# A graph layer on one Trainium2 core: message slots that run on from block to block, with a second product at each block's end

## The chip, the cores and the metric

The kernel runs on one core of a Trainium2 chip. A core has five engines that run their own instruction streams: TensorE (PE, matrix products; its weight loads are shown apart as PEld), VectorE (DVE), ScalarE (ACT), GpSimd (POOL) and SyncE (SP, which here only issues transfers). Sixteen DMA engines move data between the chip's memory (HBM) and the core's working memory (SBUF). TensorE writes its products to a second, small memory (PSUM), which VectorE and ScalarE read. Instructions of different engines wait for one another by semaphores.

The metric is the time of one execution on the device in microseconds, the median of several runs. Lower is better.

## The reference, cut to what matters

All arrays are fp32. `x` has 12,500 nodes of 256 values; `src` and `dst` are 200,000 edges, sorted by `dst`. `dst` is drawn as floor(12500 u^2) with u uniform, so low nodes have many edges and high ones few.

```
xn = layernorm(x)
h = xn
for layer in 0, 1, 2:                      # weights Wl, Wr: 256 x 256
    s   = segment_sum(h[src], dst)         # sum of the messages of each node
    cnt = number of edges of each node
    h   = (s / max(cnt, 1)) @ Wl.T + bl + h @ Wr.T
    if layer < 2: h = leaky_relu(h, 0.01)
x = x + log_softmax(h) + linear_attention(xn)   # 4 heads of 32
x = x + moe(layernorm(x))                  # 8 experts, top 2, gelu, 256 wide
```

The part that the change touches is `segment_sum(h[src], dst)`: 200,000 rows of 256 values are fetched by index and added up by destination, three times.

## The kernel before

**Blocks, slots and the sums.** The nodes are cut into 98 blocks of 128. A *slot* is a list of up to 128 edges that all have their destination in one block. For each slot the kernel does three things: GpSimd issues an indirect DMA that fetches the 128 source rows of 1 KB into a message buffer (`gather`, L978); VectorE makes a 128 x 128 matrix of zeros and ones, edge against node of the block, four slots in one instruction (`make_hots`, L970); and TensorE multiplies that matrix with the messages and adds the result to the block's sums in PSUM (`product`, L993). The last slot of a block is padded with edges that point past the end, so the slots of a block begin anew with each block: with 98 blocks there are at most 1659 (`NS`). Blocks are taken in falling order, the last one (fewest edges) first.

**Which block a slot belongs to is data.** The program is written out for a fixed number of slots, and the place of a slot's sums comes from a table in SBUF (`where`, `where1`), which TensorE's sequencer reads into registers eight slots at a time (`addresses`, `AHEAD` = 8). The sums of 4 (layer 0) or 6 (layers 1 and 2) blocks are held in a ring in PSUM. When a block's sums are complete is not known when the program is written: `ends_by` (L88) gives, from the distribution of `dst` and a margin of 4.5 standard deviations, a slot number `due[r]` by which block r is surely done, and at that slot `take_up(r)` (L1004) has VectorE read its sums, divide by the counts, and clear the ring's place. `last = due[-1]` (L931) is 1626, so that many slots a layer are run. If the data breaks one of these bounds, a flag (`other`) sends the kernel down a slower branch, `one_by_one` (L888), which makes no assumption.

**The order in a layer** is written out by hand in `on_the_way_of` (L955; under `manual_schedule`): for each slot s, `gather(s)`, every fourth slot a `make_hots` for three groups of four ahead, `product(s)`, then loads of the previous results (`load_z`) and `take_up` where due, and then as much other work as a credit allows (`SHARE` = 0.7, 0.5 and 1.0 us of TensorE a slot in layers 0, 1 and 2). The other work is generators that yield their cost: in layer 0 the keys, values and context of the attention (`first_products`, which loads xn), in layer 1 the attention's output (`attended`, which loads xT), in layers 0 and 1 the products with the weights for the blocks taken up (`products`, `linear`), and in layer 2 the softmax, the router and the experts (`expert_steps`: p_h at L835, gelu L837, p_y L804). What is left when the slots are over runs behind the last product. The last group of layer 2 needs its own softmax (`softmaxed`) and transposes (p_tr, L519) before its experts.

**Message buffers.** There are `MSGS` = 32, each a tile of its own. Gather s writes buffer s mod 32 and may not start before the buffer's earlier readers are done. For slots from 32 on this is reduced to one wait every fourth slot, by hand:

```
            if s >= MSGS:
                last_reader = [made_of[s - MSGS + FEW - 1]] if s % FEW == 0 else []
```

(L981 to L982): gather s waits for the product of slot s - 29, and the rest of the dependencies that the framework would find are declared away. For the first 32 slots of a layer the framework's own dependencies stand, which with 32 separate tiles are those on the layer before.

**Setup.** Before the first layer, `edges`, a table of (source, destination) pairs, is written to HBM; samples of it, every 128th edge, are read back (`samp_i`), and from them the first edge of each block is searched for (p_lt, an indirect read `near`, p_st); counts of slots and their running sum give `where` (p_blk, L407 to L413). For 13 chunks of 128 slots, VectorE works out each slot's first edge, GpSimd fetches the 128 edges of each slot by an indirect DMA (`got`, L449), TensorE transposes sources and destinations (p_t), and VectorE copies them to `src_of` and `dst_of` (L457 to L459). Between these stand the layernorms of x (`first_norm`, L206), ten groups of four blocks before the tables and fifteen after, whose results go to HBM as the source of layer 0's gathers. Six more VectorE instructions on the `where` tables stand at the start of `on_the_way` (L938 to L944).

**Queues.** SyncE issues nearly all the loads and stores, in program order; ScalarE's queue carries the edge sources, the weights and the stores of the normed x; GpSimd's carries the indirect transfers.

## Time and profile before

| | value |
|---|---|
| median of 3 timed runs | 7560.73 us (7558.60 to 7565.72) |
| profiled execution, its own time | 6887.68 us |
| span in the profile | 6885.9 us |
| mean granted TensorE clock | 0.815 |
| TensorE busy | 5885.1 us, 85% |
| GpSimd busy | 4857.7 us, 71% |
| VectorE, ScalarE busy | 31%, 12% |
| HBM read and written | 765.16 MB, 130.01 MB |
| setup | 0 to 178 us |
| layer 0 | 178 to 2267 us |
| layer 1 | 2293 to 4393 us |
| layer 2 | 4414 to 6827 us |
| rest | 6827 to 6885.9 us |

The profiled execution is shorter than the timed ones; the parts of the table below the first row all belong to that one execution. The layers' borders are the first and the last gather of a layer for layers 0 and 1, and the last product for layer 2.

How to read the lines of the profile: a group of instructions has its source line, its engine, its operation, what it writes and reads (out<-in), the shape, and the count; then the busy time, the mean of one in ns, and the engine's idle time just before these instructions with what ended most of it. "issue" as the releaser means that the engine waited for nothing that the profile shows. In a table by stretches each row is a window of time with the busy time and number of instructions of each engine in it. In lists in order of time the columns are start, duration, engine, line, operation, and in brackets the idle time before it and its releaser. The granted clock (PEclk) is a share of TensorE's full speed.

### The profile page before, as it was taken

What the parts mean: (1) busy time and instruction counts of PE and PEld (TensorE: products, weight loads), DVE (VectorE), ACT (ScalarE), POOL (GpSimd) and SP (SyncE); (2) the same over time, 40 slices, a digit from 0 to 9 for tenths busy, and PEclk for the clock granted to TensorE, in tenths of its full rate; (3) what the DMA queues carried; (4) which work ended last, traced back from release to release, by engine and by line L of the source; (5) the groups of instructions that cost most, each with busy time, mean ns of one, the idle gap of its engine ahead of it and who ended that gap; (6) DMA issues with size and microseconds to landing.
All of it is one profiled execution on the core that took longest, in us unless ns stands there. A gap on an engine that the chain in (4) does not pass through costs nothing.

```text
span 6885.9 us, 59263 instructions
## 1 busy us (share of the span) xinstructions
PE 5885.1 (85%) x18905; PEld 3700.0 (54%) x18905; DVE 2139.6 (31%) x5121; ACT 850.9 (12%) x1444; POOL 4857.7 (71%) x5004
## 2 busy tenths in 40 slices
PE   1788888888889777788888888889999999999998
PEld 0566666443343445543344333366666667676776
DVE  7333333221111233322211111134434444343433
ACT  0111111000000000000000000022222222222221
POOL 1777777777777677777777777666666666666663
PEclk9999999676665788866666655589999999999999
DMA  6655555443333566644444333443434433333332
GB/s 189 186 162 168 168 172 165 121 120 112 112 111 104 150 185 183 190 137 120 121 120 122 112 107 108 107 121 117 125 116 126 119 113 115 118 113 110 108 110 62
DMA packets 477361, 899.44 MB, mean 131 GB/s; under 512 B 90244, under 2 KB 305805, under 8 KB 476803
## 3 DMA queue, kind: packets, MB, share of 16 engines
q0 software_dynamic: 234832, 641.49, 32.8%
q1 hardware_dynamic: 225110, 234.04, 10.6%
q10 hardware_dynamic: 17114, 19.99, 0.9%
q8 instruction: 174, 2.85, 0.2%
q14 instruction: 131, 1.07, 0.0%
HBM read 765.16 MB, written 130.01 MB: 130 GB/s over the span
## 4 chain that ended last, share of the span: by engine, by line
PE 54%; POOL 18%; issue 12%; DMA 11%; DVE 4%; ACT 1%; SPq 0%; DVEq 0%; POOLq 0%; ACTq 0%
PE acc L993 20%; POOL msg L978 18%; PE p_h L835 10%; PE p_y L804 10%; DMA msg<-y,src_of 7%; PE p_mm L191 4%; PE p_tr L519 2%; DMA xn<-y 2%; PE p_a L661 1%; PE p_l L537 1%; PE p_b L752 1%; PE p_z L597 1%; PE p_r L708 1%; PE p_k L570 1%; DMA xt<-in_x 1%
## 5 line engine op out<-in xcount | busy, mean ns | idle before, releaser
L978 POOL DMA_INDIRECT msg<-y,src_of x4878 | 4837.9, 992 | 1818.3 <-issue 1292.8
L993 PE MATMUL acc<-msg,hots 128*128 128x256 f32 (+1 forms) x9756 | 3601.7, 489 | 523.0 <-DMA msg<-y,src_of 416.8
L993 PEld LDWEIGHTS acc<-msg,hots 128*128 128x128 f32 x9756 | 2019.4, 230 | 2070.6 <-DMA msg<-y,src_of 1188.0
L970 DVE TENSOR_TENSOR hots<-cols,dst_of 128x512 f32<-128x512 f32 (+1 forms) x1221 | 842.1, 690 | 2990.3 <-PE acc L993 2989.3
L835 PE MATMUL p_h<-turned,w_sb 128*128 128x512 f32 (+1 forms) x1600 | 769.7, 606 | 0.0
L804 PE MATMUL p_y<-w_sb,hT 128*128 128x256 f32 x3136 | 741.1, 379 | 0.1
L804 PEld LDWEIGHTS p_y<-w_sb,hT 128*128 128x128 f32 x3136 | 595.8, 190 | 81.5 <-ACT hT L837 0.5
L521 ACT COPY turned<-p_tr 128x512 f32<-128x512 f32 (+1 forms) x250 | 142.8, 578 | 3333.9 <-PE p_tr L519 3312.2
L791 DVE SCALAR_TENSOR_TENSOR x<-p_y,comb,x 128x256 f32<-128x256 f32 x784 | 341.2, 476 | 576.8 <-PE p_y L804 576.8
L835 PEld LDWEIGHTS p_h<-turned,w_sb 128*128 128x128 f32 x1600 | 317.5, 199 | 221.5 <-issue 197.1
L837 ACT ACTIVATE hT<-p_h,b_sb 128x512 f32<-128x512 f32 (+1 forms) x400 | 271.6, 679 | 1173.0 <-PE p_h L835 1172.2
L191 PE MATMUL p_mm<-wlr_sb,turned 128*128 128x512 f32 x784 | 392.8, 629 | 0.3 <-ACT turned L521 0.2
L191 PEld LDWEIGHTS p_mm<-wlr_sb,turned 128*128 128x128 f32 x784 | 157.6, 203 | 127.3 <-issue 105.9
L1018 DVE SCALAR_TENSOR_TENSOR h<-acc,inv_w,h 128x256 f32<-128x256 f32 x196 | 94.7, 483 | 233.2 <-PE acc L993 229.8
L661 PE MATMUL p_a<-m_sb,xT 128*128 128x256 f32 x392 | 126.0, 479 | 24.2 <-DMA xT<-xT_tab 24.2
L519 PE MATMUL p_tr<-ident,xn 128*128 128x128 f32 x196 | 47.3, 401 | 113.7 <-DMA xn<-y 113.7
L180 DVE TENSOR_TENSOR yz<-p_mm,bl_sb 128x256 f32<-128x256 f32 x196 | 82.2, 419 | 194.6 <-ACT yz L179 194.6
L179 ACT COPY yz<-p_mm 128x256 f32<-128x256 f32 x196 | 73.0, 373 | 520.6 <-PE p_mm L191 506.4
L519 PE MATMUL p_tr<-ident,h 128*128 128x128 f32 x392 | 74.0, 319 | 71.0 <-DVE h L1028 45.1
L661 PEld LDWEIGHTS p_a<-m_sb,xT 128*128 128x128 f32 x392 | 97.8, 252 | 47.9 <-issue 25.3
L837 ACT ACT_TABLE_LOAD x70 | 89.8, 1283 | 230.0 <-PE p_h L835 229.1
L519 PEld LDWEIGHTS p_tr<-ident,h 128*128 128x128 f32 x392 | 55.5, 163 | 94.7 <-DVE h L1028 55.8
(197 smaller groups left out, 2251.7 us busy)
## 6 DMA issues: line engine op xcount, KB each, us to landing
msg<-y,src_of POOLq DMA_INDIRECT x4878, 2.8
h<-z SPq DMA_DIRECT2D x72, 512.0 KB
y<-yz SPq DMA_DIRECT2D x98, 256.0 KB
z<-yz SPq DMA_DIRECT2D x98, 256.0 KB
y<-o_norm ACTq DMA_DIRECT2D x24, 512.0 KB
xn<-y SPq DMA_DIRECT2D x24, 512.0 KB
xT_tab<-turned SPq DMA_DIRECT2D x24, 512.0 KB
z<-z SPq DMA_DIRECT2D x24, 512.0 KB
```

Of the source, the lines that this page charges most:

```text
L191: nc.tensor.matmul(p, hT[:, k, j * P:(j + 1) * P], w[:, k, :], start=(k == 0), stop=(k == 1))
L519: nc.tensor.transpose(p_tr[:, j * P:(j + 1) * P], t[:, j, k * P:(k + 1) * P], ident)
L521: nc.scalar.copy(tT[:, k, :n * P], p_tr[:, :n * P])
L661: nc.tensor.matmul(p[:, j - j0, :], xT[:, k, j * P:(j + 1) * P], m2_sb[:, k, :], start=(k == 0), stop=(k == 1))
L791: nc.vector.scalar_tensor_tensor(xt[:, j, :], p[:, j - j0, :], comb[:, j, i:i + 1], xt[:, j, :], op0=OP.mult, op1=OP.add)
L804: nc.tensor.matmul(p[:, j - j0, :], hT[:, k, j * P:(j + 1) * P], e.w2[:, i, k, :], start=(k == 0), stop=(k == 1))
L835: nc.tensor.matmul(p_h[:, :n * P], e.w1[:, i, k, m * P:(m + 1) * P], tT[:, k, :n * P], start=(k == 0), stop=(k == 1))
L837: nc.scalar.activation(hT[:, m, :n * P], p_h[:, :n * P], AF.Gelu, bias=e.b1[:, i, m:m + 1])
L970: nc.vector.tensor_tensor(hot[:, :n, :], cols.rearrange("p (o c) -> p o c", o=1).to_broadcast([P, n, P]), dst_of[:, s:s + n].rearrange("p ...
L978: got = nc.gpsimd.indirect_dma_start(out=msgs[s % MSGS][:, :D], out_offset=None, in_=y_tab[layer], in_offset=bass.IndirectOffsetOnAxis(ap= ...
L993: got = nc.tensor.matmul(acc[:, bass.ds(at[s % AHEAD], w)], hots.pop(s), msgs[s % MSGS][:, :w], start=False, stop=True, skip_group_check=True)
L1018: got = nc.vector.scalar_tensor_tensor(h, sums_of(r), inv[:, r:r + 1], h, op0=OP.mult, op1=OP.add)
```

## The change

**Slots run on.** A slot is now 128 consecutive edges of the sorted list, whichever blocks they belong to: `NSF` = 200000/128 rounded up = 1563 a layer, where 1626 were run. A slot belongs to the block of its first edge in the order of work. Where a block ends inside a slot, the edges of the next block in that slot are added by a second product: `make_hot_end(r)` builds a one-hot matrix of that slot against block r + 1 (VectorE, made some 8 slots ahead, three buffers), and `product_end(r)` multiplies it with the slot's messages into the sums of r + 1. Which slot that is is data too: the second product reads its messages at an address from a register (table `where_end`), so the message buffers are now one tile `msgs` with 48 places. There are 97 second products a layer, in the program behind the product of slot `due[r] - 1`, ahead of the taking up of that block.

**Bounds.** `due`, `lowest` and `highest` are worked out anew for such slots (`end_of`); the flag now checks three conditions for every slot: its block is at least `lowest`, at most `highest`, and at most one more than that of the slot before.

**Waits of the gathers.** From slot 48 on, a gather of every fourth slot waits for the product of the slots that last used its four buffers and, where a second product could have read them last (`first_reuse`), for that second product. Below slot 48 the framework's own dependencies stand, as before below 32.

**Tables.** Slots being consecutive edges, the edges of a chunk are read by one direct load on SyncE's queue, in reverse order of slots, and put in order by a product with a flipped identity in place of the transpose; the block of a slot is its first destination divided by 128. The tables `where` and `where_on` come from that by arithmetic on one row, the flag by three comparisons on one row, and the ends' tables from counts (p_nr, p_nc) and one indirect read (`end_got`). The search for the blocks' first edges, the per-slot block numbers and the 13 indirect reads now belong to the other branch (`slots_by_block`). `edges` has a block of padding in front as well. One of the two copies of each transposed piece is now ScalarE's. The memsets of `due_sb` on GpSimd become those of `lowest_sb` and `highest_sb`.

```diff
-MSGS = 32
+MSGS = 48
...
-    due = [min(ends_by(r + 1), NS) for r in range(NB)]
+    NSF = (E + P - 1) // P
+    due = [min(math.ceil(end_of(r + 1, 1)), NSF) for r in range(NB)]
...
+        for c in range(NCF):
+            n = min(P, NSF - c * P)
-            got = work.tile([P, P, 2], I32, name="got")
-            nc.gpsimd.indirect_dma_start(
-                out=got.rearrange("p c t -> p (c t)"), out_offset=None, in_=edges,
-                in_offset=bass.IndirectOffsetOnAxis(ap=of_i[:, 0:1], axis=0))
+            got = work.tile([P, P, 2], I32, name="got", bufs=4)
+            nc.sync.dma_start(got[:n], edges[P + E - P * (c * P + n):P + E - P * P * c, :]
+                              .rearrange("(q e) t -> q e t", e=P))
...
+            nc.scalar.copy(got_f[:n, 0, :], got[:n, :, 0])
...
+                nc.tensor.matmul(p_t[:, :n], got_f[:n, t, :], flip[:n, P - n:], start=True,
+                                 stop=True)
+                (nc.scalar.copy if t else nc.vector.tensor_copy)(to[:, c * P:c * P + n], p_t[:, :n])
+            p_row = psum.tile([1, P], F32, name="p_row", tag="p_sm")
+            nc.tensor.matmul(p_row[:, :n], ahead[:n, c:c + 1], flip[:n, P - n:], start=True,
+                             stop=True)
+            nc.vector.tensor_copy(row[:, c * P:c * P + n], p_row[:, :n])
...
+        nc.vector.tensor_copy(row_i, row[:, :NSF])
+        nc.vector.tensor_scalar(part, row_i, RING[0] - 1, None, op0=OP.bitwise_and)
+        nc.vector.tensor_scalar(where[:, :NSF], part, 2.0 * D, None, op0=OP.mult)
...
+        off = sort.tile([1, 3, NSF], F32, name="off")
+        nc.vector.tensor_tensor(off[:, 0], row[:, :NSF], lowest_sb, OP.is_lt)
+        nc.vector.tensor_tensor(off[:, 1], row[:, :NSF], highest_sb, OP.is_gt)
...
+        nc.vector.tensor_reduce(any_off, off.rearrange("p t s -> p (t s)"), AX.X, OP.max)
...
     def take_messages(lists, n):
 
-        msgs = [lists.tile([P, W], F32, name=f"msg{i}") for i in range(n)]
-        for msg in msgs:
-            nc.vector.memset(msg[:, D:], 1.0)
+        msgs = lists.tile([P, n, W], F32, name="msgs")
+        nc.vector.memset(msgs[:, :, D:], 1.0)
         return msgs
...
-        last = due[-1]
+        last = NSF
...
         def gather(s):
             got = nc.gpsimd.indirect_dma_start(
-                out=msgs[s % MSGS][:, :D], out_offset=None, in_=y_tab[layer],
+                out=msgs[:, s % MSGS, :D], out_offset=None, in_=y_tab[layer],
                 in_offset=bass.IndirectOffsetOnAxis(ap=src_of[:, s:s + 1], axis=0))
             if s >= MSGS:
-                last_reader = [made_of[s - MSGS + FEW - 1]] if s % FEW == 0 else []
+                last_reader = []
+                if s % FEW == 0:
+                    last_reader = [made_of[min(s - MSGS + FEW, last) - 1]]
+                    last_reader += [made_of[-1 - r] for r, f in enumerate(first_reuse)
+                                    if s <= f < s + FEW]
...
+        def make_hot_end(r):
+            ends[r] = work.tile([P, P], F32, name="hot_end", bufs=3)
+            nc.vector.tensor_scalar(ends[r], cols, dst_end[:, r:r + 1], None, op0=OP.is_equal)
+
+        def product_end(r):
+
+            nonlocal at_end
+            if r % AHEAD == 0:
+                at_end = addresses(where_end, r, NB, MSGS, PE, W)
+            got = nc.tensor.matmul(sums_of(r + 1), ends.pop(r),
+                                   flat[:, bass.ds(at_end[r % AHEAD], w)], start=False, stop=True,
+                                   skip_group_check=True)
+            tc.declare_no_dep(got.ins, group=evicts,
+                              reason="only blocks that are not yet taken up are added to")
+            tc.add_to_no_dep_group(products_at, got.ins)
+            made_of[-1 - r] = got.ins
...
             product(s)
+            for i in range(NB - 1):
+                if due[i] == min(s + 8, last):
+                    if i not in ends:
+                        make_hot_end(i)
+            for i in range(NB - 1):
+                if due[i] == s + 1:
+                    product_end(i)
```

## The prediction

> **What bounds the kernel now.** I read the costliest groups first, to see which two engines could set the end; then the busy time by stretches, cut at the layers; then the order of time on GpSimd and on TensorE at the layers' ends and starts.
>
> The costliest groups of the page (busy us, mean ns of one, then idle time before and its main releaser):
>
> ```profile
> L978 POOL DMA_INDIRECT msg<-y,src_of x4878 | 4837.9, 992 | 1818.3 <-issue 1292.8
> L993 PE MATMUL acc<-msg,hots 128*128 128x256 f32 (+1 forms) x9756 | 3601.7, 489 | 523.0 <-DMA msg<-y,src_of 416.8
> ```
>
> 4878 gathers are 3 x 1626. GpSimd's idle time is mostly "issue": between gathers it waits for nobody. The stretches of the three layers and of the end (busy us and instructions of each engine, granted TensorE clock, DMA share, GB/s):
>
> ```profile
> core 0: us, PE busy (x) PEld busy (x) DVE busy (x) ACT busy (x) POOL busy (x), PEclk, DMA share, GB/s
> 178.00:2267.00 2089.00, 1757.70 (x5767) 1085.43 (x5768) 554.83 (x1205) 170.28 (x343) 1592.28 (x1626) 0.79 0.48 141
> 2293.00:4393.00 2100.00, 1726.07 (x4216) 912.61 (x4216) 476.54 (x800) 63.81 (x144) 1604.71 (x1626) 0.70 0.47 138
> 4414.00:6827.00 2413.00, 2309.98 (x8651) 1647.59 (x8652) 960.26 (x2470) 583.96 (x884) 1639.72 (x1626) 0.93 0.39 115
> 6827.00:6886.00 59.00, 36.23 (x147) 29.25 (x146) 16.03 (x51) 16.92 (x31) 0.00 (x0) 0.80 0.06 18
> ```
>
> Layers 0 and 1 take the same time although their TensorE work differs (5767 against 4216 records): 2089/1626 = 1.285 and 2100/1626 = 1.292 us a slot. Layer 2 takes 1.48, with TensorE 96% busy at a clock of 0.93. GpSimd in order of time, at the end of layer 0:
>
> ```profile
> 2265.17 0.94 POOL L978 DMA_INDIRECT msg<-y,src_of  x1 [0.30 <-issue]
> 2266.42 0.95 POOL L978 DMA_INDIRECT msg<-y,src_of  x1 [0.30 <-issue]
> 2293.07 0.94 POOL L978 DMA_INDIRECT msg<-y,src_of  x1 [25.71 <-DMA z<-yz]
> ```
>
> 0.95 + 0.30 = 1.25 us a gather, and no wait but the one for the next layer's rows. So layers 0 and 1 are GpSimd's, layer 2 TensorE's, and the first 178 us are the tables'. How long a gather takes to land, and TensorE at a layer's quiet start, in its dense part, at layer 1's start and at the very end (records of a product come in pairs):
>
> ```profile
> DMA to landing us min/median/max: 2.6/2.8/8.7
> ```
>
> ```profile
> 4437.30 17.33 PE L993 MATMUL acc<-msg,hots 128*128 128x256 f32 x28 [0.17 <-DMA msg<-y,src_of]
> ...
> 4511.14 1.03 PE L993 MATMUL acc<-msg,hots 128*128 128x256 f32 x4
> ...
> 2321.11 3.75 PE L661 MATMUL p_a<-m_sb,xT 128*128 128x256 f32 x8 [5.23 <-DMA xT<-xT_tab]
> ...
> 6841.12 0.75 PE L519 MATMUL p_tr<-ident,o 128*128 128x128 f32 x2 [13.72 <-DVE o L171]
> ```
>
> A product takes 1.24 us (17.33/14) where TensorE follows the gathers, 0.43 where it is dense (4511.14 to 4512.00 is two).
>
> **What the Trainium skill says.** "TensorE: Matmul & The Clock Gate", Part 1: a little-used TensorE passes half its clock pulses; the 0.70 to 0.79 of layers 0 and 1 against 0.93 agree. "DMA: Bandwidth & Descriptors", Anatomy of one DMA: 2.0 us and bytes/436e3 for a transfer that GpSimd issues; an estimate of 2.3 us for 128 rows of 1 KB, where the trace has 2.8, which I use. "SBUF — State Buffer", Who interferes with whom: VectorE in its two-port modes shuts GpSimd out; the first gathers of layer 0 last 1.28, 2.65, 1.68 and 5.86 us while VectorE works without a gap (177 to 190 us).
>
> **The change, part by part.**
>
> *Gathers.* 1626 to 1563: 63 fewer a layer. Layers 0 and 1: 63 x 1.285 + 63 x 1.292 = -162 us. Layer 2: nothing, TensorE sets it.
>
> *Second products.* 97 a layer against 63 slots dropped: 34 more products. In layers 0 and 1 hidden under the gathers: TensorE has 332 and 374 us of idle time there, and a 1.24 us product speeds up as TensorE gets denser. In layer 2: 34 x 0.43 = +14.6. The extra 97 one-hots on VectorE (0.2 to 0.7 us each, from the 128x512 hots' 0.69) hide in a VectorE that is 23 to 40% busy. Without that cover, 97 x 0.69 = 67 us a layer.
>
> *A new wait.* The message buffer is now one tile, and the second product reads it at an address from a register, so it counts as a reader of all 48 messages. Gathers from slot 48 on are freed of this by a declaration; the first 48 are not (the branch begins at `s >= MSGS`). So the gathers of slots 8, 16, 25, 33 and 42 of each layer, those that follow a second product in the order of the program, wait for it. Each costs: landing of the gather before 2.8, its product 1.22, second product 1.22, start 0.3, less the usual 1.25: 4.3 us; at least 2.65 (0.67 and 0.43 for the products), at most 9.5 where TensorE stands before a late load of 5.2 us as at 2321 us. All later gathers are queued behind on GpSimd, so in layers 0 and 1 it is lost. Layer 0: 5 x 4.3 + one late load 5 = +26.5. Layer 1: two late loads, +31.5. Layer 2: +21.5, since before slot 43 no expert work is there to fill TensorE. Sum +79.5; bounds 15 x 2.65 = 40 and 15 x 9.5 = 142.
>
> From slot 48 on a gather may lead by 26 to 48 slots, before by 29 to 32: nothing, landing takes 2.8 us, three slots.
>
> *Due slots.* The first group of layer 2 is taken up at slot 33, not 39; the first p_h stands after 43 products, before after 49: 6 x 1.25 = -7.5.
>
> *The end of layer 2.* Expert work is spread by slots, and there are fewer: 48 p_y (0.43 each) and 20 p_h (0.86), 38 us, move behind the last product, ahead of the last group's p_tr. They fill its 13.72 us wait: -14. (If the last softmax starts late too: 0.)
>
> *Tables.* Gone: the search (74 to 92 us), the 13 indirect reads with their replies (3.5 to 7 us each in the chain), the per-slot block numbers. New: 13 direct reads on SP's queue ahead of the last 11 loads of x, 7 VectorE instructions a chunk (about 1.46 us, 19 in all), and work on one partition: 1x1659 instructions took 1.0 us, with two inputs 1.88; six, one and three give 13.5, and a maximum over 4,689 elements 4.9 (an estimate from 0.48 for 320): 18. So 37 us against the some 35 that go; the norms stay. Only idle time can be saved: VectorE was idle 14 of the 66 us from 92 to 158. I take -8; bounds -20 and +15. The six `where` instructions (177.2 to 184.2) leave the start of layer 0, where four gathers took 12.7 us in place of 5.0: -5 (0 to -8).
>
> *Sum:* -162 + 14.6 + 79.5 - 7.5 - 14 - 8 - 5 = -102 us, on the profiled execution's 6887.7 (span 6885.9): 6785. The median of the timed runs, 7560.7, is 673 us longer, and the trace can't show where. If those us lie in the gathers of layers 0 and 1 (0.2 us each), the gain is 26 us larger; if in TensorE's layer 2, 2 to 3 smaller. I take -110: **7450 us**, its own range 7415 to 7485.
>
> **Rivals.**
>
> *The new waits are short* (2.65 us, late loads not met): 40 less than 79.5, and with the tables' -20 the time is 7450 - 52 = 7398. For it: TensorE speeds up when dense. Against: after each wait it is idle, and at half clock.
>
> *The new waits are long* (10 us each): +70, 7520. For it: xT and xn loads of 5 us or more come in the first 60 us of layers 0 and 1. Against: layer 2 has none there. Break-even at (102 + 79.5)/15 = 12.1 us a wait.
>
> *TensorE sets all three layers in the timed runs*, the side that is slower. If what makes them 673 us longer is TensorE, the 102 more products cost 102 x 0.43 to 0.86 = +44 to +88, the waits at the starts some 40 more, the smaller terms -35: 7610 to 7655. It decides from where TensorE's work for a slot passes 1.285 us; it is busy 84 and 82% in layers 0 and 1, so from a fifth more. For it: TensorE already runs nearly gapless late in layer 0. Against: there it is slow because it waits, and has twice the clock to gain; and no gather waits for it. Should it set layer 0 alone beside layer 2, layer 0 loses its 81 us and pays 14.6: 7546, no change.
>
> *The change doesn't run*: the new flag would send the kernel down the other branch. Worked out from the reference's inputs (its seed), none of the 1563 slots breaks the three conditions: 0.01.
>
> **How the numbers follow.** Forecast 0.52, short waits 0.16, long waits 0.12, TensorE in all layers 0.10, in two 0.05, flag 0.01, the rest 0.04 for tables that grow. Range 7380 to 7550: the forecast's own, the short and the long waits and TensorE in two layers, less what leaves out the other cases and some edges. Faster: 0.52 + 0.16 + 0.10 of the long waits + 0.02 = 0.80; slower: TensorE in all layers, flag, 0.02 of the long waits, 0.01 of the rest = 0.14; same 0.06. A measurement tells 0.2% (15 us) from no change.
>
> **What would show it.** Layers 0 and 1 at 1.25 us a gather and some 55 us shorter each; five idle stretches of GpSimd released by the product in each layer's first 70 us, 3 to 10 us long, and none after; layer 2 about as long as before; no 14 us wait before the last p_tr; the first gather near 170 us. Wrong if the five stretches are missing or pass 12 us, if gathers wait for products later in a layer, or if layer 2 grows by over 30 us.

## The result, and the profile after

In the timed runs on record the changed kernel took **7899.51 us** (median of 6, 7882.29 to 7914.04), the kernel before 7560.06 (6 runs, 7553.98 to 7571.73, three of them those of the table of before): a ratio of 1.0446, with a 95% interval of 1.0430 to 1.0462. It is slower by 340 us where 110 less were forecast, and it lies outside the forecast's 7380 to 7550.

Its profile is of an execution of 7903.47 us (span 7900.3), so for once the page shows what the timed runs measured. Its costliest groups, the ones that answer to the two shown of before, with the second products (L1126) as a third:

```profile
L1087 POOL DMA_INDIRECT msgs<-y,src_of x4689 | 4659.9, 994 | 2964.3 <-issue 1341.1
L1106 PE MATMUL acc<-msgs,hots 128*128 128x256 f32 (+1 forms) x9378 | 2807.5, 431 | 936.5 <-issue 341.6
...
L1126 PE MATMUL acc<-msgs,hot_end 128*128 x582 | 198.0, 424 | 186.0 <-DVE hot_end L1119 104.7
```

The counts are as forecast: 4689 gathers are 3 x 1563, 582 records of second products are 2 x 97 x 3. A gather still takes 0.99 us. But GpSimd now stands idle 2964 us ahead of gathers, of which 1341 are the 0.30 us of issue; before it was 1818 with 1293. And TensorE, idle 936 us ahead of the products, has "issue" as its main releaser: time in which it waited for nothing that the profile shows. By stretches (setup, the three layers, what is left behind the last product):

```profile
core 0: us, PE busy (x) PEld busy (x) DVE busy (x) ACT busy (x) POOL busy (x), PEclk, DMA share, GB/s
...
177.00:2646.00 2469.00, 1569.99 (x5841) 1120.50 (x5842) 555.34 (x1249) 170.32 (x343) 1554.32 (x1563) 0.78 0.39 116
2666.00:4968.00 2302.00, 1291.61 (x4258) 895.34 (x4257) 478.03 (x876) 63.43 (x144) 1570.23 (x1563) 0.73 0.41 123
4995.00:7817.00 2822.00, 2417.77 (x8584) 1684.15 (x8585) 947.65 (x2525) 573.48 (x874) 1534.73 (x1563) 0.87 0.32 95
7817.00:7901.00 84.00, 72.90 (x282) 54.06 (x280) 26.96 (x77) 26.37 (x43) 0.00 (x0) 0.94 0.06 19
```

All three layers are longer than before (2089, 2100 and 2413), with 63 slots fewer; and in layers 0 and 1 the engines are *less* busy than before, GpSimd (1554 of 2469) and TensorE (1570 of 2469) alike. VectorE's and ScalarE's busy times there are within 2 us of those before. What ended GpSimd's idle time, from the waits of the whole execution (us, times, longest):

```profile
POOL msgs L1087 <- issue: 1341.1, 4359, 7.2
POOL msgs L1087 <- PE acc L1126: 1073.7, 129, 33.9
POOL msgs L1087 <- remote: 259.0, 72, 48.7
```

129 gathers wait for a second product, up to 34 us. 15 such waits, at the layers' starts, were forecast. The other waits of layer 0 sit at slots such as 96 and 136, and the program has them: at slot 96 the gather waits for the second product that stands behind slot 58's. That is 38 slots back, within the lead that the prediction had counted (26 to 48). The wait is no surprise; that GpSimd sees TensorE 38 slots behind is.

**Where TensorE was.** A stretch of layer 0 in order of time, all engines, just before the gather of slot 96 (at 344.72):

```profile
312.87 1.11 PE L636 MATMUL p_tr<-ident,xn 128*128 128x128 f32 x4 [18.66 <-issue]
...
314.67 1.06 PE L636 MATMUL p_tr<-ident,xn 128*128 128x128 f32 x4
...
328.60 0.69 DVE L1079 TENSOR_TENSOR hots<-cols,dst_of 128x512 f32<-128x512 f32 x1 [21.57 <-remote]
...
338.44 0.59 ACT L638 COPY turned<-p_tr 128x512 f32<-128x512 f32 x1 [31.87 <-remote]
339.07 0.50 PEld L687 LDWEIGHTS p_k<-turned,wk_sb 128*128 128x128 f32 x2 [23.22 <-ACT turned L638]
...
340.63 0.59 ACT L638 COPY turned<-p_tr 128x512 f32<-128x512 f32 x1 [1.61 <-remote]
```

TensorE's transposes start at 312.87 and 314.67 and would be over by 315.7; ScalarE, which needs them, copies the first four at 338.44 and the others at 340.63, and TensorE waits for these copies. "remote" as a releaser means that the profile found no instruction which ended at that moment. The end of a product is modelled in these lines; what is recorded is the count of TensorE's semaphore, which goes up when a product is done, in e4_after 0.4 to 0.6 us behind its start. In this stretch the trace has it going up at

```
recorded execution of the changed kernel (ten counts due from products started 312.87 to 315.95):
  318.77  322.97  328.57  332.07  334.18  336.97  338.37
  340.47  340.51  340.54  340.57  340.61  340.65
the same ten instructions in e4_after, below (started 285.65 to 288.75):
  286.14  286.36  286.57  286.78  287.68  287.89  288.11  288.32  288.54  289.29
```

So the instructions start on TensorE at the usual pace, 0.21 us apart, and their counts come late: for 20 us they are 1.4 to 5.6 us apart, in multiples of 0.70 us, and then six come within 0.18 us. ScalarE's two copies start 0.07 and 0.02 us behind a count, so the count is late for those who wait for it, and not only on paper. **TensorE's counts come late**, here by up to 24 us, while its granted clock was on record as full or half. Everything else follows: VectorE and ScalarE wait for it, it waits for them, and once the gathers are 38 slots ahead GpSimd stands too. Gaps of over 10 us between the products of two slots: 28, 35 and 16 in the three layers, 1633 us in all, up to 54 us; the profile of before has 1, 12 and 1, at most 23 us. Where this document says that TensorE is held back, it means this: its counts come late, whatever holds them.

That the products themselves ran slow is not shown, and the counts speak against it. In the recorded execution 1357 of TensorE's 7234 counts come within 0.05 us of the count before, mostly 0.034 us, up to 19 in a row; in none of the other nineteen traces of this case are two of them less than 0.108 us apart. Counts that are held up and then let go together look like that; products do not end so close to one another.

A second thing sets this execution apart: much of the record of the counts is missing from its trace. The same program leaves, in the two executions,

| counts on record | recorded execution | e4_after |
|---|---|---|
| TensorE | 7,234 | 8,692 |
| VectorE | 3,653 | 4,710 |
| ScalarE | 892 | 1,202 |
| DMA transfers | 24,688 | 84,956 |

For VectorE only the record is lacking, and the counts were made in time: its next instruction begins 0.035 us (median) after the one it waited for, whether that one's count is on record or not. So the releasers that the profile names for this execution are to be read with care. The first line of the stretch shows it: the transposes wait for the load of xn, as they do in e4_after below, and the profile says "issue". Late counts and missing records begin together, some 200 us into the execution, last to about 7800 of its 7900 us, and stand in no other trace. Whether recording the counts is itself what holds them up is a rival that no run here tests.

The profile of before shows none of this. Its execution took 6887.68 us and the timed runs 7560: the 673 us that the prediction could not place. That the timed runs of before had the same trouble is the plain reading, but no profile of an execution of 7560 us exists. The trouble was steady: the six timed runs of each kernel agree within 0.4%. In all the sets of runs that follow TensorE was free of it, and both kernels' times agree with their profiles.

### The profile page after: what moved, and what is told of

Same layout as the page of the kernel before. It is cut to its first block, busy times and chain, and to the rows that moved or that the text cites. A ratio compares the mean times of both kernels' runs of the same rounds, so it can differ in the third digit from the quotient of the medians.

```text
span 7900.3 us, 59163 instructions
## 1 busy us (share of the span) xinstructions
PE 5409.5 (68%) x19177; PEld 3789.9 (48%) x19177; DVE 2140.3 (27%) x5238; ACT 855.4 (11%) x1472; POOL 4671.6 (59%) x4895
## 4 chain that ended last, share of the span: by engine, by line
PE 51%; another core or an unknown queue 22%; issue 11%; POOL 5%; DMA 4%; DVE 4%; ACT 1%; SPq 0%; ACTq 0%; DVEq 0%; POOLq 0%
PE acc L1106 20%; PE p_h L952 9%; PE p_y L921 9%; POOL msgs L1087 5%; PE p_mm L218 4%; PE p_tr L636 2%; DMA msgs<-y,src_of 2%; PE acc L1126 1%; PE p_b L869 1%; DMA xn<-y 1%; PE p_l L654 1%; DMA xT<-xT_tab 1%; PE p_a L778 1%; PE p_z L714 1%
## 5 line engine op out<-in xcount | busy, mean ns | idle before, releaser
L1087 POOL DMA_INDIRECT msgs<-y,src_of x4689 | 4659.9, 994 | 2964.3 <-issue 1341.1
L1106 PE MATMUL acc<-msgs,hots 128*128 128x256 f32 (+1 forms) x9378 | 2807.5, 431 | 936.5 <-issue 341.6
L1106 PEld LDWEIGHTS acc<-msgs,hots 128*128 128x128 f32 x9378 | 1926.4, 214 | 1778.7 <-issue 825.6
L1079 DVE TENSOR_TENSOR hots<-cols,dst_of 128x512 f32<-128x512 f32 x1173 | 805.8, 691 | 3429.2 <-remote 1417.9
L921 PE MATMUL p_y<-w_sb,hT 128*128 128x256 f32 x3136 | 777.6, 389 | 96.4 <-issue 49.4
L952 PE MATMUL p_h<-turned,w_sb 128*128 128x512 f32 (+1 forms) x1600 | 793.3, 619 | 24.5 <-issue 20.8
L218 PE MATMUL p_mm<-wlr_sb,turned 128*128 128x512 f32 x784 | 426.1, 672 | 177.8 <-issue 94.2
L1126 PE MATMUL acc<-msgs,hot_end 128*128 x582 | 198.0, 424 | 186.0 <-DVE hot_end L1119 104.7
L1126 PEld LDWEIGHTS acc<-msgs,hot_end 128*128 128x128 f32 x582 | 121.7, 213 | 217.7 <-DVE hot_end L1119 109.0
L654 PE MATMUL p_l<-wlr_sb,turned 128*128 128x256 f32 x392 | 120.4, 459 | 49.3 <-issue 38.8
```

Of the source, the lines that this page charges most:

```text
L218: nc.tensor.matmul(p, hT[:, k, j * P:(j + 1) * P], w[:, k, :], start=(k == 0), stop=(k == 1))
L654: nc.tensor.matmul(p[:, j - j0, :], mT[:, k, j * P:(j + 1) * P], wlr_sb[:, 0, k, :D], start=(k == 0), stop=(k == 1))
L921: nc.tensor.matmul(p[:, j - j0, :], hT[:, k, j * P:(j + 1) * P], e.w2[:, i, k, :], start=(k == 0), stop=(k == 1))
L952: nc.tensor.matmul(p_h[:, :n * P], e.w1[:, i, k, m * P:(m + 1) * P], tT[:, k, :n * P], start=(k == 0), stop=(k == 1))
L1079: nc.vector.tensor_tensor(hot[:, :n, :], cols.rearrange("p (o c) -> p o c", o=1).to_broadcast([P, n, P]), dst_of[:, s:s + n].rearrange("p ...
L1087: got = nc.gpsimd.indirect_dma_start(out=msgs[:, s % MSGS, :D], out_offset=None, in_=y_tab[layer], in_offset=bass.IndirectOffsetOnAxis(ap= ...
```

## The experiments

**The kernel before, unchanged**, to see whether 673 us of difference come back.

> The kernel before, unchanged. Theory A (TensorE itself runs slow in spells: in the profile of the changed kernel its products between 316 and 338 us end 1.4 to 5.6 us apart, where 0.2 to 0.4 is usual, and VectorE, ScalarE and at last GpSimd wait for them; the profile of the kernel before, 673 us shorter than its timed runs, happened to be free of them): this time 7540 to 7590 us, and its profile, if it falls on an ordinary execution, some 670 us longer than the 6886 of before, with such spells. Theory B (the changed kernel's waits of gathers for second products make the difference, spells are their mark): the time is the same 7560, and the profile shows no products that end late.

Measured: 6890.52 us (12 runs), the runs beside it 6891.56; no late counts in its profile. The profile of before was an ordinary execution, and the 7560 of its timed runs was not. Neither theory is decided by this, but the two numbers that the forecast had put together (profile 6888, median 7560) are now known to be of different conditions.

**The change without its second products:**

```diff
-            for i in range(NB - 1):
-                if due[i] == min(s + 8, last):
-                    if i not in ends:
-                        make_hot_end(i)
-            for i in range(NB - 1):
-                if due[i] == s + 1:
-                    product_end(i)
```

> The changed kernel without its second products, their one-hot matrices and the waits for them (the edges of a slot that belong to the next block are left out of the sums); 1563 slots, 48 message places and the tables stay. Theory B: the stalls of the gathers go, 7250 to 7450. Theory A: spells of TensorE remain wherever they come from, 7750 to 7900, and the gathers wait for ordinary products instead.

Measured: 6680.48 us beside 6891.56, ratio 0.9699 (0.9683 to 0.9715). Outside both expectations, which had taken 7560 as the base.

**The change without the waits of the first 48 gathers:**

```diff
-            if s >= MSGS:
+            if True:
                 last_reader = []
-                if s % FEW == 0:
+                if s % FEW == 0 and s >= MSGS:
```

> The changed kernel with the first 48 gathers of a layer freed of waiting for the second products (the declaration is made from slot 0 on). My prediction's term: 79.5 us less, 7820. If slow TensorE is the limit (theory A), what the gathers gain at the start is not kept: 7870 to 7900.

Measured: 6750.44 us, ratio 0.9790 (0.9773 to 0.9807). Outside both expectations too, and for the same reason. With e4_after, below, this prices the waits.

**The kernel before with 63 slots a layer left out:**

```diff
-    due = [min(ends_by(r + 1), NS) for r in range(NB)]
+    bound = [min(ends_by(r + 1), NS) for r in range(NB)]
+    due = [min(d, 1563) for d in bound]
```

> The kernel before with its last 63 slots of each layer left out (the edges in them are missing from the sums), so 1563 gathers and products a layer and nothing else of the change. By my prediction's first term, 162 us less than before and some 30 for fewer products in layer 2: 7365 to 7400. If TensorE sets all layers in the timed runs, 63 products of 0.6 us a layer: 7440 to 7450.

Measured: 6682.21 us, ratio 0.9693 (0.9677 to 0.9709): 209 us less, where the first term and its share of layer 2 gave 192. From the first gather to the last, layers 0 and 1 are 77.2 and 76.6 us shorter (2088.3 and 2099.8 to 2011.1 and 2023.2), for 81 each in the forecast. Both expectations had 7560 as their base.

**The change itself, and TensorE made slower evenly.** The second and third kernel issue each product twice (and each second product): sums and counts double, the means stay.

```diff
+            hot, ready = hots.pop(s), cleared.pop(s, [])
+            for _ in range(2):
                 got = nc.tensor.matmul(acc[:, bass.ds(at[s % AHEAD], w)], hot,
```

> The changed kernel, unchanged, beside the same runs of the kernel before. If the kernel before takes 6890 us here, as in the first set of runs, TensorE is not held back, and my prediction's sum of parts (-102 us) should show: 6790; with e2_no_early at 6750 the waits at the layers' starts would then be worth 40 us, or 80 by my own price: 6790 to 6830. If the kernel before takes 7560 here, products end late again: 7900.

> The kernel before with every product of messages issued twice (sums and counts both double, so the means stay): TensorE is made slower evenly, 1626 x 0.43 = 700 us a layer more. Layer 0 comes to 1.32 us a slot and is just bound by TensorE (+50 us), layer 1 stays with the gathers, layer 2 takes all of it (+700): 7640.

> The changed kernel with every product and second product issued twice. If an evenly slower TensorE is why the changed kernel lost, its time stands to that of e5_before_twice as 7900 to 7560, 1.02 to 1.05. If it is not the amount of work but when TensorE is late, the two are within 1%: layer 1 keeps its 80 us less, layers 0 and 2 pay 2 x 34 x 0.43 = 29 us each, and the waits at the starts some 15 each.

Measured: the changed kernel takes **6811.83 us** beside 6884.88, ratio 0.9888 (0.9871 to 0.9904): with TensorE not held back it is 73 us *faster*. Its stretches, to be held against those of the recorded execution above (the kernel's lines are one higher):

```profile
179.00:2223.00 2044.00, 1724.46 (x5842) 1088.18 (x5842) 555.90 (x1249) 169.46 (x343) 1537.38 (x1563) 0.82 0.46 140
2242.00:4295.00 2053.00, 1639.36 (x4292) 911.44 (x4292) 486.20 (x882) 63.53 (x144) 1546.67 (x1563) 0.74 0.46 137
4311.00:6729.00 2418.00, 2294.87 (x8586) 1635.32 (x8587) 958.67 (x2527) 576.68 (x874) 1520.67 (x1563) 0.93 0.37 111
6729.00:6812.00 83.00, 72.13 (x280) 53.62 (x278) 26.54 (x77) 26.34 (x43) 0.00 (x0) 0.94 0.06 20
```

The same program, the same counts of instructions; the recorded execution is longer by 425, 249 and 404 us in the layers and by 1 in the rest. The granted clock differs little (0.82, 0.74, 0.93 against 0.78, 0.73, 0.87), so the clock on record doesn't tell it. The stretch of transposes again, in e4_after:

```profile
285.65 1.11 PE L637 MATMUL p_tr<-ident,xn 128*128 128x128 f32 x4 [3.81 <-DMA xn<-y]
...
286.85 0.58 ACT L639 COPY turned<-p_tr 128x512 f32<-128x512 f32 x1 [7.20 <-PE p_tr L637]
...
287.46 1.06 PE L637 MATMUL p_tr<-ident,xn 128*128 128x128 f32 x4
...
288.56 0.59 ACT L639 COPY turned<-p_tr 128x512 f32<-128x512 f32 x1 [1.12 <-PE p_tr L637]
```

The copy follows the fourth transpose at once, and is released by it. What TensorE's products waited for, first in the recorded execution, then in e4_after:

```profile
PE acc L1106 <- issue: 341.6, 141, 20.5
PE acc L1106 <- DVE hots L1079: 288.1, 30, 54.8
...
PE acc L1106 <- DMA msgs<-y,src_of: 139.4, 145, 7.1
```

```profile
PE acc L1107 <- DMA msgs<-y,src_of: 492.6, 653, 6.6
...
PE acc L1107 <- DVE hots L1080: 60.3, 8, 52.9
```

Where TensorE keeps up it waits for messages, 653 times. The 145 of the recorded execution can't be held against that: 71% of the DMA's counts have no record there, and a wait whose count has no record can be put to "issue" or to somebody else. What stays is 288 us of waits for VectorE's matrices, where e4_after has 60; and VectorE in its turn had waited for TensorE's counts, as at 328.60 us above.

The doubled products: 7673.66 us before (ratio 1.1145, 1.1126 to 1.1163), 7691.82 changed (1.1170, 1.1151 to 1.1188); the two stand at 1.0024. Longer work of TensorE, of about the size that the recorded runs show as lateness, takes the change's 73 us away, and 18 more. It does not make 340 of it. In layer 0 the kernel before pays 207 us (2295 for 2088) where 50 had been expected, in layer 2 588 where 700 had; the changed kernel keeps 24 us of layer 1's 80.

**TensorE made slower in lumps**, since the recorded lateness comes in spells; TensorE is kept at work in the lumps, so the counts behind them come late, though not in the way of the recorded execution:

```diff
+            for i in range(65 if s % 64 == 63 else 1):
+                got = nc.tensor.matmul(acc[:, bass.ds(at[s % AHEAD], w)], zeros if i else hot,
```

> The kernel before with TensorE kept busy by 64 products against a matrix of zeros (they add nothing) in one lump behind every 64th slot's product: 64 x 0.43 = 27.5 us, 24 or 25 times a layer, like the spells of 10 to 54 us in the profile of the changed kernel. The same work as in e5_before_twice, but in lumps. Gathers may run 29 to 32 slots ahead, 36 us at 1.25 us, so the lumps hold them little: 7640 to 7700, as e5_before_twice, and up to 7800 where a lump and the work waiting behind it exceed 36 us.

> The changed kernel with the same lumps. If the changed kernel loses because its gathers wait for late second products where they would not for even lateness (theory A with the lead of 26 to 38 slots at the blocks' ends as what matters), it is 2 to 5% slower than e7_before_lumps. If lateness in lumps costs both the same, it is within 1% of it, and then the loss in the timed runs comes from TensorE being held back longer in the changed kernel than in the kernel before, for a reason still to be found.

Measured: 8004.22 us before (ratio 1.1635, 1.1615 to 1.1654), 7914.65 changed (1.1498, 1.1479 to 1.1518). The kernel before is over the 7800 that had been expected at most; the two are within 1.1% of each other, the changed kernel the faster. The kernel before has 25 lumps a layer and the changed one 24, for it has fewer slots; three lumps are 3 x 27.5 = 82 us, and without them the two are level within 0.1%. The change's gathers do wait for second products there, as in the recorded profile; first the changed kernel with lumps, then the kernel before with them:

```profile
POOL msgs L1089 <- PE acc L1131: 1397.1, 122, 40.9
```

```profile
POOL msg L980 <- PE acc L997: 1371.5, 504, 33.8
```

122 long waits against 504 short ones, and nearly the same sum. So as far as the lumps stand for the recorded lateness, the second products' waits are not what loses the time: they are only the place where lateness of TensorE shows in this kernel. In the kernel before it shows at the ordinary products. What is left for the recorded runs, by subtraction, is that being held back cost the changed kernel more: 7900 - 6812 = 1088 us over its undisturbed time, against 7560.7 - 6887.7 = 673 for the kernel before.

**Both kernels again, unchanged**, in further sets of runs, and the change without its first waits, to meet TensorE's late counts a second time.

> The kernel before, for its profile, in case TensorE is held back in this set of runs. If so (7560 us): theory A has its products end late in it too, 673 us of lateness in all, with gaps over 10 us between the products of two slots in layers 0 and 1, where the profile of before has 13; and the gathers wait for products at a lead of 29. If not, 6890 as before.

> The changed kernel once more, in another set of runs. Where TensorE is not held back: 6810, with the kernel before at 6890. Where it is: 7900, with the kernel before at 7560; the record's loss then repeats, and is tied to the execution and not to the kernel alone.

> The kernel before in the same set, for its profile. Where TensorE is held back (7560): its products end late too, 673 us of it against some 1090 in the changed kernel. Where not: 6890, and no late ends.

> The kernel before once more for its profile, in another set of runs. 6890 without late products, or 7560 with 673 us of them.

> The kernel before in a last set of runs. 6890 without late products, or 7560 with them: 673 us of lateness.

> The changed kernel in the same set: 6810, or 7900 where TensorE is held back.

> The changed kernel without the first 48 gathers' waits in the same set: 6750. Where TensorE is held back: 7870 to 7900 if those waits have no part in the loss, 7560 to 7750 if they start it.

Measured: the kernel before 6885.61, 6878.11, 6885.86 and 6889.64 us; the changed one 6801.02 and 6808.63; without the first waits 6753.94. The condition was not met again in seven sets of runs, on six chips, and no profile of these has late counts or lacks records of them. On which chip the recorded runs ran is not on record. The three sets that had both kernels have the change 73, 78 and 75 us faster, the last two by one execution each.

**A layer 2 with more other work a slot**, on top of e2_no_early:

```diff
-SHARE = (0.7, 0.5, 1.0)
+SHARE = (0.7, 0.5, 1.04)
```

> The changed kernel without the waits of the first 48 gathers, as e2_no_early, and with layer 2's share of other work raised from 1.0 to 1.04 us a slot, so that the experts' work that had moved behind the last product goes back in front of it. TensorE sets layer 2 either way: 6740 to 6755 where e2_no_early took 6750. Where TensorE is held back: unknown; below 7900 if the waits at the layers' starts matter there.

Measured: 6750.74 us, ratio 0.9802 (0.9785 to 0.9818), no different from e2_no_early. The tail behind the last product goes from 83.4 to 58.4 us, and layer 2 up to there grows by 25: the wait that the moved work had filled is back (13.68 us ahead of the last group's p_tr), yet nothing is lost.

**The second products' one-hot matrices on ScalarE**, on top of e2_no_early:

```diff
-            nc.vector.tensor_scalar(ends[r], cols, dst_end[:, r:r + 1], None, op0=OP.is_equal)
+            off = work.tile([P, P], F32, name="hot_off", bufs=2)
+            nc.scalar.activation(off, cols, AF.Abs, bias=dst_end[:, r:r + 1])
+            nc.scalar.activation(ends[r], off, AF.Relu, bias=ones[:, 0:1], scale=-1.0)
```

> The changed kernel without the first 48 gathers' waits (as e2_no_early, 6750), with the second products' one-hot matrices made by two ScalarE instructions (the absolute difference, then 1 minus it cut at 0) in place of one of VectorE. e2_no_early's gathers of layers 0 and 1 took 13.0 and 10.8 us longer in all than e1_no_end's, and 38 and 44 of 97 of these matrices overlap a gather of over 1.05 us. If VectorE, busy with them, holds GpSimd up, some 20 us go: 6725 to 6735. If the longer gathers have another cause: 6745 to 6755. Where TensorE is held back it should make no difference.

Measured: 6735.66 us, ratio 0.9782 (0.9766 to 0.9799), whose interval overlaps e2_no_early's 0.9790 (0.9773 to 0.9807). The four runs lie between 6726.06 and 6755.20, so the time does not decide between the two expectations. In its trace, of the slowest of the four, layers 0 and 1 have 174 and 165 gathers of over 1.05 us, against 147 and 169 with VectorE making the matrices and 122 and 148 without second products. The long gathers have not gone with VectorE's 97 matrices; that these are not the cause is likely and not shown, and the cause stays open.

## Why the prediction was wrong, and what of it held

**The step that failed** is the last of the sum, which carries it from the profiled execution to the timed runs: "The median of the timed runs, 7560.7, is 673 us longer, and the trace can't show where. If those us lie in the gathers of layers 0 and 1 (0.2 us each), the gain is 26 us larger; if in TensorE's layer 2, 2 to 3 smaller. I take -110". Both cases keep the engine that sets each layer. What the runs showed in its place is that in the profiled one of the recorded runs TensorE is held back in spells, in layers 0 and 1 too (they are 425 and 249 us longer than undisturbed), so that all three layers, whose bounds had been read from the profile of before, have another bound there. The median and the profile that the step added up are of two conditions: undisturbed, the kernel before takes 6872 to 6898 us in every later run, and the change 73 us less (e4_after), where the sum of parts had 102 less. A profile 9% shorter than the median was not a smaller copy of the timed runs.

The rival *TensorE sets all three layers in the timed runs* came nearest to the place and was priced too low for the recorded runs: 7610 to 7655, given 0.10. It let TensorE be evenly slower, and for that its price was too high: 49 to 94 us, where e5_before_twice and e6_after_twice, evenly slower by about as much, differ by 18. Its "against" (twice the clock to gain, no gather waits for it) was read in an execution in which TensorE was not late. The 4.5% need more lateness in the changed kernel than in the kernel before, 1088 us against 673. **Why the change loses more by it is open.** More work of TensorE does not do it (e6_after_twice), nor do lumps of it, nor the gathers' lead under such lumps (e8_after_lumps); counts held up behind products that ended in time were not imitated. What holds the counts up, and whether that belongs to the chip, to the moment, to the recording or to what the kernel asks of TensorE, could not be tried, since it didn't come again.

The Trainium skill, "TensorE: Matmul & The Clock Gate", section "Seeing it yourself", warns that the clock gate's records have been unreliable on trn2 and that the clock has been seen stuck at a quarter for over 50 us. That would be a ready explanation, and the numbers do not fit it. The transposes complete 0.21 us apart at a granted clock of 0.5 and 0.11 at 1.0 (e4_after), so at a quarter they would be some 0.43 us apart (an estimate from these two), where 1.4 to 5.6 us were seen; and a slower clock would not put counts 0.034 us apart.

**The parts of the sum**, held against e4_after and the profile of before, both undisturbed (6811.5 and 6885.9 us of span, -74.4; forecast -102):

| part | forecast | measured |
|---|---|---|
| first gather (tables) | -8 | +1.5 |
| layer 0, first gather to last | -59.5 | -45.9 |
| change to layer 1 | 0 | -6.1 |
| layer 1, first gather to last | -49.5 | -48.3 |
| change to layer 2 | 0 | -4.2 |
| layer 2, first gather to last product | -9.4 | +4.1 |
| behind the last product | +24 | +24.4 |

(Layer 0's -59.5 is -81 + 26.5 - 5; layer 2's -9.4 is 14.6 + 21.5 - 7.5 - 38, the 38 us of experts' work coming back behind the last product as 38 - 14.) The 10 us at the two changes between layers stand in no term of the sum: as far as the forecast goes, they are luck.

*Fewer gathers*: 162 us forecast, 154 in e3_cut. Right.

*Second products*: 0.43 us each in layer 2, measured 40.4/97 = 0.42 (e2_no_early's 2400.0 us to the last product against e1_no_end's 2359.6). Their cover in layers 0 and 1 was to hide them; there e2_no_early is 23.5 and 11.1 us longer than e1_no_end, of which the gathers' own durations are 13.0 and 10.8. A term put at nothing that measured 35 us, whose cause e13_act_end did not find.

*The new wait at the layers' starts*: 79.5 us forecast, 61 by the medians of e4_after and e2_no_early; by layer 20, 28 and 17 where 26.5, 31.5 and 21.5 stood. The place is right to the slot. GpSimd in order of time at the start of layer 2 in e4_after; the gathers of slots 8, 16, 25, 33 and 42:

```profile
4325.55 0.94 POOL L1088 DMA_INDIRECT msgs<-y,src_of  x1 [4.20 <-PE acc L1127]
...
4339.47 0.94 POOL L1088 DMA_INDIRECT msgs<-y,src_of  x1 [4.22 <-PE acc L1127]
...
4354.59 0.94 POOL L1088 DMA_INDIRECT msgs<-y,src_of  x1 [4.18 <-PE acc L1127]
...
4368.43 0.94 POOL L1088 DMA_INDIRECT msgs<-y,src_of  x1 [4.15 <-PE acc L1127]
...
4410.44 0.94 POOL L1088 DMA_INDIRECT msgs<-y,src_of  x1 [31.05 <-PE acc L1127]
```

The first four are 4.2 us less the usual 0.3, where the step had 4.3. In layers 0 and 1 they are 3.2 to 8.6, with late loads among them, as forecast. The fifth of layer 2 is 31 us, far over the 12 that the prediction had called a sign of being wrong: it had TensorE with nothing else to do before slot 43, and that gather waits out the first group's softmax and router, for which TensorE itself stands 17.44 us. Layer 2 pays 17 us in all for its five waits, for TensorE sets that layer.

*The end of layer 2*: the work moved behind the last product, and the idle time ahead of the last group's p_tr went from 13.72 us to 1.54 in e4_after, as forecast; but the -14 was not gained. In e10_share the work is back in front, the wait too, and the time is the same. The tail is 25 us longer and layer 2 just 25 shorter without the 38 us of work: a wait that is filled gives nothing if the place where the work came from doesn't shrink by all of it. e4_after:

```profile
6764.51 0.61 PE L637 MATMUL p_tr<-ident,o 128*128 128x128 f32 x2 [1.54 <-issue]
```

*Tables*: -8 forecast, +1.5; three undisturbed executions of the changed kernel have the first gather at 179.6, 170.2 and 177.6 us, before at 178.1. GpSimd's wait for the one indirect read that is left is new in e4_after:

```profile
POOL end_got L445 <- DVE n_r L440: 117.9, 1, 117.9
```

That read goes out at 129.04 us, 21 us before the last of the 13 in the kernel before (149.79), so it does not explain why nothing was gained. The last of the norms whose rows the first gathers read starts on VectorE at 174.8 us, where it was 172.2 before: VectorE's part of the setup did not get shorter. The bounds (-20 and +15) held it. The -5 at the start of layer 0 came in part: its first four gathers take 9.3 us where they took 12.7, one of them still 5.28.

*"If gathers wait for products later in a layer"* stood among the signs of a wrong prediction. They did in the recorded execution (129 waits for second products, 1074 us, the forecast ones among them). In e4_after there are 87, 414 us, of which 361 us lie in layer 2, where TensorE sets the time anyway.

## What to carry to other kernels

Where the profiled execution is much shorter than the timed runs, settle that before any sum is made on it: look in a long one for the engine whose counts come late (counts of the semaphore long behind the modelled ends, waits of everybody for one engine), and forecast for that condition, or widen the range to hold both. Before reading who released whom, see whether the counts on record are as many as in another execution of the same program: where they are not, "issue", "remote" and the numbers of waits say little. A change that trades one engine's work for another's is worth what the engine that sets the end is worth in the runs that are timed: here 63 gathers for 97 second products gained 73 us where GpSimd set two layers, lost 18 where TensorE's products were doubled, and lost 340 in the recorded runs. And in this program a buffer that is read at an address from a register counts as read everywhere: the declaration that freed all but the first 48 gathers was worth making for those too. e2_no_early does so and is 61 us faster than the change, 2.1% faster than the kernel before wherever TensorE was not held back.

## What the runs showed of the hardware

- TensorE can start products at its usual pace while its semaphore counts them late: in the stretch shown by 24 us, 1.4 to 5.6 us apart in multiples of 0.70 us, and then in a burst 0.034 us apart, in a program on one core and with a recorded clock of 0.5 to 1.0. That execution took 1088 us of 7900 more than the same program undisturbed, and its trace lacks 17% of TensorE's counts and 71% of the DMA's. In seven later sets of runs it didn't occur, not even with TensorE kept busy (granted clock 0.98 in e5_before_twice).
- A 128x128 transpose of fp32 completes every 0.21 us at a granted clock of 0.5 and every 0.11 us at 1.0, where TensorE is dense and unhindered; a 128x256 product takes 0.43 in layer 2 (clock 0.93), also at an address from a register (0.42).
- A gather of 128 rows on GpSimd takes 0.95 us and 0.30 between two, but 122 to 174 of the 1563 in layers 0 and 1 are longer than 1.05 us. They go with VectorE's one-hot matrices of 128x512: in layer 0 of e2_no_early 460 of the 1563 gathers overlap one of these, and of the 147 long gathers 141 do. The long ones cost 43 to 67 us a layer over their 0.95.
